# The last stage of a graph network: half of the second batch norm's scaling moved into TensorE's transposing matmuls, and half of the residual added by TensorE and kept in PSUM

## The chip, the cores and the metric

The kernel runs on one core of one Trainium2 chip. The metric is the device time of one execution in microseconds. Before the change it is 2655.15 us, the median of three runs (2654.74 to 2655.41). The profile is of one further execution, with a span of 2651.3 us; all points in time below count from the start of that span.

## The reference, cut to what matters

Sixteen batches of a 1024 x 256 array `x` pass through two layers. The first layer is attention over a graph with a layer norm at its end; its output is called x1 here, and the kernel keeps it in DRAM. The second layer, whose end is what is changed, is

```python
agg = einsum('nm,bmd->bnd', A_hat, x1)              # 1024 x 1024 adjacency
h   = relu(batchnorm(agg.reshape(-1, 256) @ W1.T + b1, g1, be1))   # 512 channels
out = h @ W2.T + b2                                 # 256 channels
out = batchnorm(out, g2, be2)                       # over all 16 * 1024 rows
y   = layernorm(x1 + out.reshape(16, 1024, 256))    # over the 256 channels of a row
```

The second batch norm needs its mean and variance over all rows of all batches, so nothing can be scaled before the last batch's `out` is there. After that every value of `out` is multiplied by a scale of its channel and gets a shift of its channel added, x1 is added, and each row is normalised over its 256 channels. Everything is in 32-bit floats.

## The kernel before, in words

The tail of the kernel has two stages. In both, the order of the instructions on TensorE (PE), ScalarE (ACT) and VectorE (DVE) is the order in which the program writes them (`manual_schedule`); GpSimd (POOL) and the DMA queue of SyncE (SP) are apart.

**Second linear layer (lines 1445 to 1468).** For each batch b and each half c of the 256 output channels, TensorE multiplies `w2T` with four chunks of h (`L1456`: two column halves for each of four chunks, eight matmul calls) into a PSUM tile `po2` with the channels on the partitions and the 1024 rows of the batch along the free dimension. VectorE moves it into SBUF as `o2T[b]` with the bias added (`L1460`) and takes the statistics with two bn_stats (`L1464`). After the last batch, `coefficients2(c)` aggregates the statistics (`L1227`, DVE) and works out the scale `sg2` and the shift `sh2` on GpSimd (`L587` to `L1231`), one column of each for each c. All of `o2T`, sixteen batches, stays in SBUF.

**Final stage (lines 1473 to 1542).** Per batch:

- `scale_shift` (`L1485`): ScalarE applies scale and shift in place, one 128 x 1024 activation for each of the two halves c.
- `residual2`: four pairs of 128-row blocks. For each pair TensorE transposes four 128 x 128 blocks into a PSUM bank (`L1497`), so that rows come onto the partitions and channels along the free dimension; VectorE adds x1 to it (`L1502`, 128 x 512, result in the tile `xf` in SBUF) and takes the statistics of both row blocks (`L1504`, 128 x 256 each). The four pairs go round four PSUM banks.
- ten small GpSimd instructions (`L1510` to `L1519`) turn these statistics into `rstd` and `nmr`, the scale and shift of each row.
- `finish`: ScalarE applies them in eight 128 x 256 activations (`L1526`), the result is stored by one 1 MB DMA (`L1530`), and the x1 of the batch seven later is loaded (`L1428`).

The written order is: `scale_shift(0)`, then for each b: `residual2(b)`, `scale_shift(b + 1)`, `finish(b - 1)`; and `finish(15)` at the end. So ScalarE prepares the next batch for TensorE and then finishes the batch before. x1 is loaded seven batches ahead.

Of the kernel before, what the change touches and what calls it, by code (L numbers as in the profile page):

```python
# [10 lines left out]
F32 = mybir.dt.float32  # L11
I32 = mybir.dt.int32
AF = mybir.ActivationFunctionType
ALU = mybir.AluOpType
AX = mybir.AxisListType
PSUM = bass.MemoryType.PSUM
DRAM = bass.MemoryType.DRAM

P = 128
HALF = 512  # L20
# [495 lines left out]
def fast_path(  # L516
# [19 lines left out]
    nc = tc.nc  # L536
    B, N, C = x.shape
    H = 4
    D = C // H
    NCH = N // P  # L540
    CC = C // P
    FH = W1.shape[0]
    HC = FH // P
    scale = float((1.0 + 1e-06) / (np.sqrt(D) + 1e-06))

    const = ctx.enter_context(tc.tile_pool(name="const", bufs=1))
# [4 lines left out]
    def open_psum():  # L551

        stack = ExitStack()
        for tag in "sto":
            psum[tag] = stack.enter_context(tc.tile_pool(name=f"ps_{tag}", bufs=2, space=PSUM))
        return stack
# [3 lines left out]
    def tile_s(name):  # L560
        return psum["s"].tile([P, N], F32, tag="s", name=name)

    def tile_t(name):
        return psum["t"].tile([P, HALF], F32, tag="t", name=name)

    def tile_o(name):
        return psum["o"].tile([P, HALF], F32, tag="o", name=name)
# [7 lines left out]
    ident = const.tile([P, P], F32, name="ident")  # L575
# [95 lines left out]
    H0, H1 = slice(0, HALF), slice(HALF, N)  # L671
# [3 lines left out]
    cols = {}  # L675
# [24 lines left out]
    with (  # L700
# [10 lines left out]
        st = {}  # L711
# [404 lines left out]
        with tc.manual_schedule(engines={mybir.EngineType.PE, mybir.EngineType.Activation, mybir.EngineType.DVE}):  # L1116
# [48 lines left out]
            for j in range(len(bursts)):  # L1165
                b, u = j // PERB, j % PERB
# [30 lines left out]
            j = len(bursts)  # L1197
# [14 lines left out]


    w1T, w2T = wl["w1T"], wl["w2T"]
    bn1_st = const.tile([P, HC, 2 * B, 6], F32, name="bn1_st")
    bn2_st = const.tile([P, CC, 2 * B, 6], F32, name="bn2_st")

    def batchnorm(stats, gamma, beta, k, name):

# [15 lines left out]
    with (  # L1235
# [9 lines left out]
        def bank(name):  # L1245
            return ps8.tile([P, HALF], F32, tag="bank", name=name)

        def temps(k):
            return lambda key, name: strt.tile([P, HALF], F32, tag=f"{key}{k}", name=f"{key}_{name}")


        wS = strt.tile([P, 4, C], F32, name="wS")
# [133 lines left out]
        def scale_shift1(h, k):  # L1386
            nc.scalar.activation(  # L1387
                h, h, AF.Relu, bias=sh1[:, k : k + 1], scale=sg1[:, k : k + 1]
            )
# [3 lines left out]
        for k in range(HC):  # L1393
            ps = [bank(f"ph_{k}_{half}") for half in range(2)]
            for c in range(CC):
                for half, hs in enumerate((H0, H1)):
                    nc.tensor.matmul(
                        ps[half], w1T[:, c, k * P : (k + 1) * P], t[:, c, hs],
                        start=(c == 0), stop=(c == CC - 1),
# [11 lines left out]
        nc.gpsimd.dma_start(h_d[B - 1], ht)  # L1411

    graph.close()
    ctx.enter_context(open_psum())

# [2 lines left out]
    with tc.tile_pool(name="o2p", bufs=1) as o2p:  # L1420
        o2T = [
            o2p.tile([P, CC, N], F32, tag=f"o2_{b}", name=f"o2_{b}") for b in range(B)
        ]
        xf = {}

        def load_x1(b, pool, tag):
            xf[b] = pool.tile([P, NCH, C], F32, tag=tag, name=f"xf_{b}")
            nc.sync.dma_start(xf[b], x1_d[b])  # L1428

        coefficients2, sg2, sh2 = batchnorm(bn2_st, cols["g2"], cols["be2"], CC, "bn2")  # L1430
        with (
            tc.tile_pool(name="hl", bufs=2) as hl,
            tc.manual_schedule(
                engines={mybir.EngineType.PE, mybir.EngineType.Activation, mybir.EngineType.DVE}
            ),
        ):
            hs_of = {0: h0}

            def load_h(b):
                ht = hl.tile([P, HC, N], F32, tag="hl", name=f"hl_{b}")  # L1440
                nc.sync.dma_start(ht, h_d[b])
                hs_of[b] = [ht[:, k, :] for k in range(HC)]

            load_h(1)
            for b in range(B):
                if b + 2 < B:
                    load_h(b + 2)
                if b + 1 < B:
                    for k in range(HC):
                        scale_shift1(hs_of[b + 1][k], k)  # L1450
                h = hs_of.pop(b)
                for c in range(CC):
                    ps = tile_s(f"po2_{b}_{c}")
                    for k in range(HC):
                        for hs in (H0, H1):
                            nc.tensor.matmul(  # L1456
                                ps[:, hs], w2T[:, k, c * P : (c + 1) * P], h[k][:, hs],
                                start=(k == 0), stop=(k == HC - 1),
                            )
                    nc.vector.tensor_scalar(  # L1460
                        o2T[b][:, c, :], ps, cols["b2"][:, c : c + 1], None, ALU.add
                    )
                    for half, hs in enumerate((H0, H1)):
                        nc.vector.bn_stats(bn2_st[:, c, 2 * b + half, :], o2T[b][:, c, hs])  # L1464
                    if b == B - 1:
                        coefficients2(c)
                if b >= B - 3:
                    load_x1(b - (B - 3), xp, "x")

        with (
            tc.tile_pool(name="fin2", bufs=4) as fin2,
            tc.manual_schedule(
                engines={mybir.EngineType.PE, mybir.EngineType.Activation, mybir.EngineType.DVE}
            ),
        ):
            for b in range(3, 7):
                load_x1(b, fin2, "xf")  # L1480

            def scale_shift(b):
                for c in range(CC):
                    o = o2T[b][:, c, :]
                    nc.scalar.activation(  # L1485
                        o, o, AF.Identity, bias=sh2[:, c : c + 1], scale=sg2[:, c : c + 1]
                    )

            def residual2(b):
                xt = xf[b]  # L1490
                st = small.tile([P, NCH, 6], F32, tag="ln_st", name=f"st_l1_{b}")
                for pair in range(NCH // 2):
                    pt = tile_t(f"pf_{b}_{pair}") if pair % 2 else tile_o(f"pf_{b}_{pair}")
                    for j in range(2):
                        n = 2 * pair + j
                        for c in range(CC):
                            nc.tensor.transpose(  # L1497
                                pt[:, j * C + c * P : j * C + (c + 1) * P],
                                o2T[b][:, c, n * P : (n + 1) * P], ident,
                            )  # L1500
                    xs = xt[:, 2 * pair : 2 * pair + 2, :].rearrange("p n c -> p (n c)")
                    nc.vector.tensor_add(xs, pt, xs)  # L1502
                    for n in (2 * pair, 2 * pair + 1):
                        nc.vector.bn_stats(st[:, n, :], xt[:, n, :])  # L1504

                me, qe, mo, qo = (st[:, :, k] for k in (1, 2, 4, 5))
                w = small.tile([P, 4, NCH], F32, tag="ln_w", name=f"w_l1_{b}")
                rstd, nmr, dif, var = (w[:, k, :] for k in range(4))
                pool = nc.gpsimd
                pool.tensor_tensor(nmr, me, mo, ALU.add)  # L1510
                pool.tensor_tensor(dif, me, mo, ALU.subtract)
                pool.tensor_tensor(var, qe, qo, ALU.add)
                pool.tensor_scalar(var, var, 1.0 / C, EPS, ALU.mult, ALU.add)
                pool.tensor_tensor(dif, dif, dif, ALU.mult)
                pool.tensor_scalar(dif, dif, 0.25, None, ALU.mult)
                pool.tensor_tensor(var, var, dif, ALU.add)
                pool.tensor_tensor(rstd, var, mhalf, ALU.pow)
                pool.tensor_tensor(nmr, nmr, rstd, ALU.mult)
                pool.tensor_scalar(nmr, nmr, -0.5, None, ALU.mult)  # L1519
                return rstd, nmr  # L1520

            def finish(b, rstd, nmr):
                xt = xf.pop(b)
                y = o2T[b].rearrange("p c n -> p (c n)").rearrange("p (n c) -> p n c", c=C)
                for n in range(NCH):
                    nc.scalar.activation(  # L1526
                        y[:, n, :], xt[:, n, :], AF.Identity,
                        bias=nmr[:, n : n + 1], scale=rstd[:, n : n + 1],
                    )
                nc.sync.dma_start(out[b].rearrange("(n p) c -> p n c", p=P), y)  # L1530
                if b + 7 < B:
                    load_x1(b + 7, *((fin2, "xf") if 3 <= b < 7 else (xp, "x")))

            scale_shift(0)
            coeffs = {}
            for b in range(B):
                coeffs[b] = residual2(b)
                if b + 1 < B:
                    scale_shift(b + 1)
                if b:  # L1540
                    finish(b - 1, *coeffs.pop(b - 1))
            finish(B - 1, *coeffs.pop(B - 1))


# [41 lines left out]
```

## Time and profile before

The final stage is the last 114 us of the span. A batch of it, as single rows and the timeline give it:

| engine | work of a batch | rows | time of a batch |
|---|---|---|---|
| ACT | 2 activations 128 x 1024, 8 of 128 x 256 | L1485 1226 ns, L1526 585 ns | 6.20 us from one batch to the next |
| DVE | 4 adds 128 x 512, 8 bn_stats 128 x 256 | L1502 677 ns, L1504 418 ns | 1.38 us for a pair, 5.5 us |
| PE | 16 transposes 128 x 128 | L1497 395 ns | 3 to 3.5 us in a row, then a wait |
| POOL | 10 small instructions | L1517 1667 ns, the others some 200 ns | 3.7 us |
| DMA | 1 MB in, 1 MB out | | 88% busy between 2555 and 2629 us |

The durations of single instructions overlap with the start of the next of the same engine, so the steps from start to start are shorter than these means: eight activations `L1526` take 4.03 us together, that is 0.49 us each.

For one logical fp32 matmul call the trace holds two records, each with a weight load of its own; for one `transpose` call it holds one. That is seen by counting. `L1456` is called 16 x 2 x 4 x 2 = 256 times and has 512 records; `L1497` is called 16 x 4 x 2 x 2 = 256 times and has 256 records.

### The profile page before, as it was taken

Reading aid. Unit: us, or ns where it says so; the run is one execution under the profiler, and the core shown is the slowest. Engines: PE = TensorE matmul, PEld = TensorE weight load, DVE = VectorE, ACT = ScalarE, POOL = GpSimd, SP = SyncE. Lnnn points to the kernel's source line nnn. Section 1 sums busy time; section 2 is a strip of 40 time slices with the busy share of each in tenths; the row PEclk is TensorE's granted clock in tenths of the full one; section 3 lists DMA queues with packets and bytes.
Section 4 is the critical chain, followed back from the end, with each engine's and each line's share of the span. In section 5 each row is a group of like instructions: output and inputs, shape, how many; then the busy total and the mean of one; then the engine's idle time right before and its main releaser. Section 6 shows DMA issues by size and latency. Waiting matters only on the chain. (4 is left out here: it accounts for less than half of the span.)

```text
span 2651.3 us, 31994 instructions
## 1 busy us (share of the span) xinstructions
PE 2553.7 (96%) x12966; PEld 1110.1 (42%) x12966; DVE 1600.2 (60%) x2160; ACT 1126.8 (43%) x1349; POOL 336.2 (13%) x407
## 2 busy tenths in 40 slices
PE   8999999999999999999999999999999999999964
PEld 4443444444434434444444343344444444444443
DVE  5465665756656657666566576765655655533376
ACT  5363563654645636545446354410101001233368
POOL 0001000100100011001000100321222211100044
PEclk9999999999999999999999999999999999999975
DMA  4001101001011011010110110112122122353367
GB/s 143 2 9 41 33 10 41 21 22 33 9 41 33 9 41 33 10 41 3 39 33 9 41 49 1 41 64 95 80 95 95 66 92 82 137 202 143 149 222 240
DMA packets 134557, 168.94 MB, mean 64 GB/s; under 512 B 86785, under 2 KB 120065, under 8 KB 124033
## 3 DMA queue, kind: packets, MB, share of 16 engines
q1 hardware_dynamic: 129568, 116.47, 14.2%
q0 software_dynamic: 4832, 50.34, 4.6%
q8 instruction: 103, 1.69, 0.3%
q14 instruction: 54, 0.43, 0.0%
HBM read 99.36 MB, written 67.44 MB: 63 GB/s over the span
## 5 line engine op out<-in xcount | busy, mean ns | idle before, releaser
L908 ACT ACTIVATE p<-ps 128x1024 f32<-128x1024 f32 x512 | 495.7, 1020 | 179.5 <-PE ps L903 142.9
L933 DVE TENSOR_TENSOR acc<-acc,p 128x1024 f32<-128x1024 f32 x384 | 483.2, 1258 | 61.0 <-ACT p L908 32.4
L903 PE MATMUL ps<-qT,kT 64*64 64x512 f32 x4096 | 490.6, 594 | 1.4 <-ACT p L908 1.4
L924 PE MATMUL po<-p,v 64*64 64x512 f32 x4096 | 485.3, 589 | 0.0
L805 PE MATMUL pg<-wg,x 128*128 128x512 f32 x960 | 425.2, 596 | 0.0
L979 POOL TENSOR_TENSOR x<-x,o 128x512 f32<-128x512 f32 x64 | 109.5, 1711 | 1434.8 <-DVE o L974 1434.8
L924 PEld LDWEIGHTS po<-p,v 64*64 64x64 f32 x4096 | 156.7, 133 | 282.8 <-issue 282.6
L805 PEld LDWEIGHTS pg<-wg,x 128*128 128x128 f32 x960 | 177.6, 190 | 226.9 <-issue 203.3
L903 PEld LDWEIGHTS ps<-qT,kT 64*64 64x64 f32 x4096 | 146.1, 132 | 280.2 <-issue 231.5
L817 ACT ACTIVATE qT<-qT 128x512 f32<-128x512 f32 x64 | 40.3, 631 | 482.0 <-DVE qT L814 481.9
L1456 PE MATMUL po<-hl,w12T 128*128 128x512 f32 x512 | 220.3, 592 | 3.1 <-ACT hl L1387 2.3
L814 DVE SCALAR_TENSOR_TENSOR qT<-pg,para_s 128x512 f32<-128x512 f32 x64 | 43.9, 689 | 271.1 <-PE pg L805 269.8
L793 DVE SCALAR_TENSOR_TENSOR wg<-wg,adj_s 128x1024 f32<-128x1024 f32 x128 | 153.1, 1217 | 15.5 <-ACT wg L789 15.5
L784 ACT ACTIVATE wg<-crow,ccol 128x1024 f32<-128x1024 f32 x128 | 146.6, 1146 | 11.8 <-DMA crow<-c 11.8
L1456 PEld LDWEIGHTS po<-hl,w12T 128*128 128x128 f32 x512 | 97.1, 190 | 126.3 <-issue 120.5
L789 ACT ACTIVATE wg<-wg 128x1024 f32<-128x1024 f32 x128 | 135.5, 1060 | 2.6
L1387 ACT ACTIVATE hl<-hl,bn_sh,bn_sg 128x1024 f32<-128x1024 f32 x64 | 74.3, 1229 | 135.0 <-DMA hl<-h 133.6
L855 PE MATMUL pv<-kvw_s,xT 128*128 128x256 f32 x512 | 124.0, 385 | 1.6 <-ACT kT L846 1.6
L1460 DVE TENSOR_SCALAR o<-po,col_b 128x1024 f32<-128x1024 f32 x32 | 41.1, 1284 | 139.1 <-PE po L1456 139.1
L842 PE MATMUL pk<-xT,kvw_s 128*128 128x512 f32 x256 | 120.3, 592 | 0.0
L855 PEld LDWEIGHTS pv<-kvw_s,xT 128*128 128x128 f32 x512 | 94.9, 190 | 51.9 <-issue 27.6
L1286 PE MATMUL a_agg<-ahT,x1l 128*128 128x512 f32 x240 | 108.1, 593 | 1.1 <-ACT agg L1104 1.1
(151 smaller groups left out, 2625.4 us busy)
## 6 DMA issues: line engine op xcount, KB each, us to landing
h<-hw POOLq DMA_DIRECT2D x16, 2048.0 KB, 6.6
hl<-h SPq DMA_DIRECT2D x15, 2048.0 KB
x<-x POOLq DMA_DIRECT2D x16, 1024.0 KB, 4.2
x1l<-x SPq DMA_DIRECT2D x16, 1024.0 KB
xf<-x SPq DMA_DIRECT2D x16, 1024.0 KB
out_dram<-o SPq DMA_DIRECT2D x16, 1024.0 KB
x<-in_x_dram SPq DMA_DIRECT2D x15, 1024.0 KB
crow<-c SPq DMA_DIRECT2D x15, 512.0 KB
```

The source lines that it names most:

```text
L784: nc.scalar.activation(w, s["crow"], AF.Abs, bias=s["ccol"][:, n : n + 1])
L789: nc.scalar.activation(w, w, AF.Tanh, scale=0.5)
L793: nc.vector.scalar_tensor_tensor(w, w, 1.0, adj_s[:, n, :], op0=ALU.subtract, op1=ALU.mult)
L805: nc.tensor.matmul(ps, xt[:, n, c * P : (c + 1) * P], s["wg", n][:, hs], start=(n == 0), stop=(n == NCH - 1),)
L842: nc.tensor.matmul(ps, kvw_s[:, c, kc * P : (kc + 1) * P], s["xT"][:, c, hs], start=(c == 0), stop=(c == CC - 1),)
L855: nc.tensor.matmul(pt[:, j * C : (j + 1) * C], s["xT"][:, c, n * P : (n + 1) * P], kvw_s[:, c, C : 2 * C], start=(c == 0), stop=(c == CC - 1),
L903: nc.tensor.matmul(ps[kh * D : (kh + 1) * D, hd * HALF : (hd + 1) * HALF], kT[r, pr, ks], qT[r, pr, qh * HALF : (qh + 1) * HALF], start=Tr ...
L908: nc.scalar.activation(p, ps, AF.Exp)
L924: nc.tensor.matmul(g["po"][kh][hd * D : (hd + 1) * D, :], s["v"][r, m, h * D : (h + 1) * D], p[r, hd * HALF : (hd + 1) * HALF], start=(m = ...
L933: nc.vector.tensor_add(g["acc"], g["acc"], p)
L979: nc.gpsimd.tensor_tensor(xs, xs, o.rearrange("p n h d -> p n (h d)"), ALU.add)
L1456: nc.tensor.matmul(ps[:, hs], w2T[:, k, c * P : (c + 1) * P], h[k][:, hs], start=(k == 0), stop=(k == HC - 1),)
```

## The change

It takes work off ScalarE and VectorE in the final stage and gives it to TensorE.

- **Scaling.** Only the channel half c = 0 is still scaled and shifted by ScalarE. For c = 1 the matmul that brings a block into row order has, in place of the identity, a diagonal matrix `dsg` of the scales. The shift of these channels comes from a matmul of a row of ones with the row of shifts (`one`, 1 x 128, and `row`, 1 x 256 for the two blocks of a pair), accumulated in the same PSUM bank. `dsg` and `row` are made once, in `shift_row`.
- **No more transpose calls.** Since the results accumulate, all sixteen block movements are now `nc.tensor.matmul` calls in place of `nc.tensor.transpose`, also those with the identity.
- **Residual.** For pairs 2 and 3 of each batch TensorE adds x1 by a matmul of the identity with x1 (`add_x1`, 512 columns), in the same bank. The sum stays in PSUM: bn_stats and the finishing activations of these four row blocks read it there. Pairs 0 and 1 are added by VectorE as before.
- **PSUM.** The pools of the stage before are closed; three tiles of two banks hold sums (`ps_held`), and pairs 0 and 1 go round two banks (`ps_sum`) where four pairs went round four.
- **The end of the linear layer.** The last tile of `out` (b = 15, c = 1) is moved by ScalarE in two halves in place of one VectorE instruction.

```diff
-                    nc.vector.tensor_scalar(
-                        o2T[b][:, c, :], ps, cols["b2"][:, c : c + 1], None, ALU.add
-                    )
+                    if b == B - 1 and c == CC - 1:
+                        for hs in (H0, H1):
+                            nc.scalar.activation(
+                                o2T[b][:, c, hs], ps[:, hs], AF.Identity,
+                                bias=cols["b2"][:, c : c + 1],
+                            )
+                    else:
+                        nc.vector.tensor_scalar(
+                            o2T[b][:, c, :], ps, cols["b2"][:, c : c + 1], None, ALU.add
+                        )
...
+        part_psum.close()
...
+            tc.tile_pool(name="ps_held", bufs=3, space=PSUM) as ps_held,
+            tc.tile_pool(name="ps_sum", bufs=2, space=PSUM) as ps_sum,
...
+            def shift_row():
+                nc.vector.tensor_scalar(dsg, ident, sg2[:, 1:2], None, ALU.mult)
+                pr = ps_sum.tile([P, HALF], F32, tag="sum", name="prow")
+                nc.tensor.matmul(pr[0:1, :P], sh2[:, 1:2], ident, start=True, stop=True)
+                for j in range(2):
+                    nc.vector.tensor_copy(row[:, j, :], pr[0:1, :P])
+
             def scale_shift(b):
-                for c in range(CC):
-                    o = o2T[b][:, c, :]
-                    nc.scalar.activation(
-                        o, o, AF.Identity, bias=sh2[:, c : c + 1], scale=sg2[:, c : c + 1]
-                    )
+                o = o2T[b][:, 0, :]
+                nc.scalar.activation(o, o, AF.Identity, bias=sh2[:, 0:1], scale=sg2[:, 0:1])
+
+            def add_x1(b, pair):
+                if b not in held:
+                    held[b] = ps_held.tile([P, N], F32, tag="held", name=f"held_{b}")
+                nc.tensor.matmul(
+                    held[b][:, (pair - 2) * HALF : (pair - 1) * HALF], ident,
+                    xf[b][:, 2 * pair : 2 * pair + 2, :].rearrange("p n c -> p (n c)"),
+                    start=True, stop=False, skip_group_check=True,
+                )
+
+            def transposed(b, pair, pt, start):
+                nc.tensor.matmul(
+                    pt.rearrange("p (n c) -> p n c", c=C)[:, :, P:], one, row,
+                    start=start, stop=False, skip_group_check=True,
+                )
+                for c in (1, 0):
+                    for j in range(2):
+                        n = 2 * pair + j
+                        nc.tensor.matmul(
+                            pt[:, j * C + c * P : j * C + (c + 1) * P],
+                            o2T[b][:, c, n * P : (n + 1) * P], dsg if c else ident,
+                            start=(start and c == 0), stop=True, skip_group_check=True,
+                        )
...
-                for pair in range(NCH // 2):
-                    pt = tile_t(f"pf_{b}_{pair}") if pair % 2 else tile_o(f"pf_{b}_{pair}")
-                    for j in range(2):
-                        n = 2 * pair + j
-                        for c in range(CC):
-                            nc.tensor.transpose(
-                                pt[:, j * C + c * P : j * C + (c + 1) * P],
-                                o2T[b][:, c, n * P : (n + 1) * P], ident,
-                            )
+                for pair in range(2):
+                    pt = ps_sum.tile([P, HALF], F32, tag="sum", name=f"pf_{b}_{pair}")
+                    transposed(b, pair, pt, True)
                     xs = xt[:, 2 * pair : 2 * pair + 2, :].rearrange("p n c -> p (n c)")
                     nc.vector.tensor_add(xs, pt, xs)
                     for n in (2 * pair, 2 * pair + 1):
                         nc.vector.bn_stats(st[:, n, :], xt[:, n, :])
+                for pair in range(2, 4):
+                    if b:
+                        add_x1(b, pair)
+                    pt = held[b][:, (pair - 2) * HALF : (pair - 1) * HALF]
+                    transposed(b, pair, pt, False)
+                    for j in range(2):
+                        nc.vector.bn_stats(st[:, 2 * pair + j, :], pt[:, j * C : (j + 1) * C])
...
+            add_x1(0, 2)
+            add_x1(0, 3)
             scale_shift(0)
+            shift_row()
```

`finish` takes the four blocks of pairs 2 and 3 first, from PSUM, then the other four from SBUF. Two tables of statistics, `bn1_st` and `bn2_st`, are moved to other SBUF pools.

## The prediction

> **What bounds the kernel now.** I first looked at the engines' busy time in stretches of the tail, because TensorE's 96% of the whole span says nothing of a stage in which it works otherwise. The columns are PE, weight loads, DVE, ACT, POOL, the granted TensorE clock, the DMA's share and its GB/s:
>
> ```profile
> 2531.70:2537.20 5.50, 0.21 (x1) 0.02 (x1) 3.58 (x4) 0.05 (x1) 1.36 (x5) 0.81 0.81 301
> 2537.20:2549.00 11.80, 7.64 (x43) 6.30 (x43) 9.38 (x21) 5.72 (x5) 3.44 (x10) 0.79 0.52 218
> ...
> 2555.00:2629.00 74.00, 44.60 (x192) 37.11 (x192) 65.65 (x145) 74.00 (x121) 41.26 (x120) 0.60 0.88 297
> 2629.00:2640.30 11.30, 2.65 (x16) 2.24 (x15) 6.50 (x15) 8.79 (x18) 6.87 (x20) 0.58 0.62 207
> 2640.30:2651.30 11.00, 0.00 (x0) 0.00 (x0) 0.00 (x0) 3.98 (x8) 0.00 (x0) 0.50 0.48 159
> ```
>
> From 2555 to 2629 us ScalarE is busy without a gap (74.00 of 74.00); TensorE is busy 60% of the time, and at a mean clock of 0.60. The chain of waits agrees: through this stretch it runs on ACT alone, and `L1526` starts at 2586.27 and again at 2592.47, so a batch costs **6.20 us**, which is eight `L1526` (0.49 each) and two `L1485` (1.13 each from start to start). Who waited for whom shows the other side:
>
> ```profile
> PE pf L1497 <- ACT o L1485: 40.4, 27, 6.5
> POOL w_l L1510 <- DVE st_l L1504: 40.2, 16, 8.0
> ```
>
> TensorE waits 40.4 us for the scaled tile. So taking one `L1485` of each batch away does shorten what paces the stage, as long as TensorE, which gets the work, stays under 6.20 us for a batch. Whether it does decides the case, so I price it from the timeline of TensorE (start, time to the last end, records):
>
> ```profile
> 1553.48 1.88 PE L842 MATMUL pk<-xT,kvw_s 128*128 128x512 f32 x4
> 1555.19 1.89 PE L855 MATMUL pv<-kvw_s,xT 128*128 128x256 f32 x8
> 1556.92 0.59 PE L842 MATMUL pk<-xT,kvw_s 128*128 128x512 f32 x1
> ...
> 1820.09 1.02 PE L1318 MATMUL c_h<-agg,wS 128*128 128x512 f32 x2
> 1821.05 0.19 PE L1343 MATMUL pgood<-top,ones 128*1 128x2 f32 x2
> 1821.16 2.41 PE L1286 MATMUL a_agg<-ahT,x1l 128*128 128x512 f32 x5
> ...
> 2544.26 0.66 PE L1497 MATMUL pf<-ident,o 128*128 128x128 f32 x4 [0.72 <-DVE xf L1502]
> 2555.42 3.46 PE L1497 MATMUL pf<-ident,o 128*128 128x128 f32 x15 [0.66 <-ACT o L1485]
> ```
>
> Four records of 512 columns step from 1553.48 to 1555.19: **0.429 us** a record. Eight of 256 columns step to 1556.92: **0.216 us**. The steps go with the columns, so 128 columns are 0.110; a single transpose record, also 128 columns, steps by 0.109 to 0.110 at full clock. At half clock (2555.42) it is (3.46 - 0.42) / 14 = 0.217. The middle three lines price a change of shape in the array: from the first `c_h` to `pgood` it is 0.96 us where two records would be 0.86, so some **0.093 us** are lost when a 128*1 weight follows a 128*128 one; on the way back 0.11 us pass from `pgood` to `a_agg`, of which the two little records use 0.03.
>
> **What the Trainium skill says.** "FP8 and Floating Point Precision", TensorE Precision Notes: true fp32 takes four passes through the array. The trace agrees: a matmul call is two records, each 512 columns in 0.429 us, which is 2.01 cycles a column at the page's 2.4 GHz; a transpose call is one. "Perfetto Trace Analysis", Optimizing Tensor Performance, Transposes: a logical transpose should be a transpose, not a standard matmul; the trace has both forms, at 1 and at 2 records a call. "TensorE: Matmul & The Clock Gate", step-by-step of a matmul: a weight load is pulled ahead of running matmuls unless row groups conflict; the 0.093 us at `pgood` fits a load that was not pulled ahead, though no 1-row weight occurs before. The same page, on the clock gate: the clock halves after an idle window of some 3.4 us and returns after a busy one; the 0.60 above is such a case.
>
> **The change part by part.** *ScalarE*: one `L1485` less a batch, 6.20 - 1.13 = 5.07 us. The activations reading PSUM I cost like those reading SBUF (copies from PSUM, `L937`, 586 ns for 512 columns; in SBUF, `L817`, 631 ns). *VectorE*: two pairs at 1.38 us as now, and four bn_stats from PSUM at 0.38 to 0.48 (the 0.418 of `L1504` and some for PSUM): 4.3 to 4.7 us in place of 5.5. *GpSimd* keeps its 3.7 us. *DMA* moves the same bytes.
>
> *TensorE*, a batch at full clock:
> - 16 block matmuls, each now two records: 32 x 0.110 = 3.52 us (before: 16 x 0.110 = 1.76).
> - 4 shift rows, 256 columns, two records: 8 x 0.216 = 1.73.
> - 2 `add_x1`, 512 columns, two records: 4 x 0.429 = 1.72.
> - 4 times into the 1-row weight of `one` and back: 8 x 0.093 = 0.74. This is the unknown: at best 0, since no 1-row weight is in the trace. I take the full value, because the three narrow kinds seen (128*1, 128*32, 64*64) all lose it beside 128*128.
>
> Sum **7.71 us** (6.97 without the last term). Weight loads: their records are 190 ns, longer than 110. I take them as hidden, because records of matmuls follow transposes after 0.109 us (`L765` to `L805`, 28 times) though their load is also recorded as 190. If they were not, 32 x 0.08 = 2.6 us would be added.
>
> So TensorE becomes the bound: 7.71 against ScalarE's 5.07 and the 6.20 that pace the stage now. Both waits that could stop it are covered: `scale_shift(b + 1)` waits on ACT behind `finish(b - 2)`, which waits for GpSimd some 5 us after TensorE has left batch b - 2, a batch and more before it is needed; and the third held tile is free long before. As it is busy without a break I take the full clock, but for one half-clock window at the start (1.7 us lost; 0 to 3.4).
>
> *The head.* The last matmul of `L1456` ends at about 2531.7. Before, `L1460` (1.29) and two `L1464` (1.30) follow; now the first ACT half can start on the first bank, and half a copy and two bn_stats lie in the chain: some 1.1 us less, so `sh2` comes at 2536.0 in place of 2537.1. Then, in place of a 1.25 us `L1485`, one small matmul, two copies of 1 x 128 and their waits: 0.8 to 1.5, I take 1.2. TensorE starts at 2537.2 (before 2538.45). `add_x1(0)` lies in the wait ahead of it; so does `dsg`.
>
> *The sum.* TensorE ends at 2537.2 + 16 x 7.71 - 1.72 + 1.7 = 2660.5. Two bn_stats and the end of the matmul follow (1.1): 2661.6. From the last bn_stats to the end it was 2635.8 to 2651.3 = 15.5 (GpSimd, eight activations, the last store) and stays so. The end is at 2677.1, against 2651.3: **+25.8 us, 2681.0 us**.
>
> **The rivals.**
> - *TensorE bound, the shift row costs nothing extra.* 16 x 0.74 = 11.8 less: 2669. For it: the load of a 1-row weight may go to a row group that is handled otherwise than a narrow column group.
> - *Weight loads exposed*, or the clock often at half. 16 x 2.6 = 41 more: 2722. Against: the 0.109 steps, and a clock of 1.0 wherever TensorE ran matmuls without a break.
> - *TensorE stays hidden, the kernel is faster.* If calls with a diagonal or identity cost one record like transposes, the batch would be some 4.3 us of TensorE and ScalarE would pace at 5.07. 13 of the saved `L1485` lie behind the first `finish`: 13 x 1.13 = 14.7, with 1.1 from the head, and some 2 given back at the end, where the last chain of TensorE, DVE and GpSimd (10.6 us from `scale_shift(15)` to `finish(15)`) doesn't shrink as much as ACT's work: 2641. For it: 40.4 us of waiting on TensorE. Against: every matmul call in the trace has two records.
>
> **How the numbers follow.** TensorE bound with the switches 0.56, without 0.22, loads exposed or a low clock 0.09, hidden 0.10, and 0.03 for a mixture that ends near no change. The prediction is the first, 2681. The range runs from the second less its cold start and a shorter head (2663) to the first with half a microsecond of waits in each batch and a little over (2697). Slower 0.87, same 0.03, faster 0.10.
>
> **What would show it.** In the changed profile TensorE should be busy near 100% from about 2537 to 2660 at clock 1.0; the block matmuls have 512 records, the rows 128, `add_x1` 64, and a batch 7.7 us from one to the next. ScalarE should fall to two thirds and wait for GpSimd, GpSimd for DVE, DVE for TensorE. A gap of 0.2 where `one` is loaded and no more than 0.110 between blocks confirm the terms. ScalarE still without gaps, or single records for the block matmuls, would prove me wrong.

## The result, and the profile after

The changed kernel takes 2718.64 us (median) against 2655.19 before: a ratio of 1.0238, 95% interval 1.0218 to 1.0258. It is **63.5 us slower**. One of the four timed runs, 2778.02 us at a lower mean clock (0.968 against 0.992 and 0.993), was in a slower state and is left out of the ratio. The direction was forecast and so was the engine that becomes the bound; the size was not: 25.8 us were predicted, and the range ended at 2697.

The stretches of the tail, read as before (PE, weight loads, DVE, ACT, POOL, granted clock, DMA share, GB/s), with who waited for whom after them (in total, times, longest):

```profile
2540.00:2560.00 20.00, 19.15 (x66) 13.11 (x65) 7.30 (x16) 4.05 (x9) 3.47 (x10) 0.57 0.17 72
2560.00:2580.00 20.00, 18.29 (x96) 11.74 (x94) 8.82 (x20) 6.91 (x13) 6.86 (x20) 1.00 0.61 201
...
2680.00:2700.00 20.00, 18.29 (x96) 11.74 (x94) 8.82 (x20) 8.82 (x17) 6.86 (x20) 1.00 0.32 107
```

```profile
ACT o L1575 <- POOL w_l L1568: 97.2, 16, 21.0
DVE st_l L1553 <- PE held L1531: 66.3, 32, 3.3
...
PE held L1517 <- DVE st_l L1553: 12.8, 15, 0.9
```

ScalarE, which had no gap before, now idles 97.2 us in the stage; VectorE waits 66.3 us for TensorE; the DMA share falls from 88% to between 61% and 65% from 2560 to 2640 us. So TensorE is the bound. But it isn't busy without a break: 18.29 of 20 us, and in the first stretch its clock is 0.57. The third wait says who stops it, 15 times (in batch 0, whose `add_x1` ran ahead, the shift matmul of pair 3 waits instead). One batch of the timeline, from the first shift matmul of pair 0 to that of the next batch, shows all of it (TensorE's lines, and VectorE's one that matters):

```profile
2603.23 0.69 PE L1524 MATMUL pf<-row,one 1*128 1x256 f32 x2
...
2603.86 0.71 PE L1531 MATMUL pf<-dsg,o 128*128 128x128 f32 x4
...
2604.40 0.61 PE L1531 MATMUL pf<-ident,o 128*128 128x128 f32 x4
...
2604.94 0.69 PE L1524 MATMUL pf<-row,one 1*128 1x256 f32 x2
...
2608.69 0.61 PE L1531 MATMUL held<-ident,o 128*128 128x128 f32 x4
2609.34 0.76 DVE L1553 BATCH_NORM_STATS2 st_l<-held 128x6 f32<-128x256 f32 x2 [1.10 <-PE held L1531]
...
2610.15 1.12 PE L1517 MATMUL held<-xf,ident 128*128 128x512 f32 x2 [0.85 <-DVE st_l L1553]
...
2611.21 0.69 PE L1524 MATMUL held<-row,one 1*128 1x256 f32 x2
...
2612.92 0.69 PE L1524 MATMUL pf<-row,one 1*128 1x256 f32 x2
```

From 2603.23 to 2612.92 a batch takes **9.69 us**, not 7.71. The records are the forecast ones: two for each matmul call, four in the `dsg` group and four in the `ident` group of a pair. Two things are larger. A shift matmul starts at 2603.23 and the block after it at 2603.86, 0.63 us for two records whose columns take 0.43. And `add_x1` of pair 3 starts at 2610.15, just after VectorE has finished the statistics of pair 2 (2609.34 + 0.76), though it writes another bank. The starts of single records give the terms of the batch:

| term | predicted us | measured us | how measured |
|---|---|---|---|
| 32 block records | 3.52 | 3.58 | 0.112 from one to the next |
| 8 shift records, columns | 1.73 | 1.73 | 0.216 where nothing else delays them (second experiment) |
| 4 add_x1 records | 1.72 | 1.72 | 0.431 and 0.429 |
| change of the weight's shape | 0.74 | 1.56 | at each shift matmul four steps too long: 0.205 for 0.110 into it, 0.320 for 0.216 between its records, 0.304 for 0.216 behind it, 0.213 for 0.112 between the first two block records |
| wait for VectorE | 0 | 1.12 | 1.129 in place of 0.111 into the second add_x1, 0.533 in place of 0.431 within it |
| sum | 7.71 | 9.71 | 9.69 from batch to batch |

The head did not go as forecast either:

```profile
2528.54 3.17 PE L1457 MATMUL po<-hl,w12T 128*128 128x512 f32 x7
...
2530.34 3.50 ACT L1510 ACTIVATE o<-o,bn_sh,bn_sg 128x1024 f32<-128x1024 f32 x3 [13.14 <-POOL bn_sh L1229]
...
2533.75 1.24 ACT L1463 ACTIVATE o<-po,col_b 128x512 f32<-128x512 f32 x2
2534.44 1.29 DVE L1472 BATCH_NORM_STATS2 bn_st<-o 128x6 f32<-128x512 f32 x2 [5.91 <-ACT o L1463]
...
2538.36 0.19 POOL L1229 TENSOR_TENSOR bn_sh<-col_be,bn_sh 128x1 f32<-128x1 f32 x1
...
2539.56 0.69 PE L1524 MATMUL pf<-row,one 1*128 1x256 f32 x2 [0.57 <-DVE row L1506]
```

TensorE's last linear matmul ends at 2531.7, but the two ACT halves (`L1463`) start at 2533.75. On ACT they stand behind three `scale_shift` activations, of batches 0, 1 and 2: across the two stages the order of the built program is not that of the text. The shift is there at 2538.55, not at 2536.0, and TensorE starts at 2539.56, not at 2537.2. From 2542.1 to 2559.1 it then runs at half clock, 17.1 us, where one window of 3.4 was forecast. It is busy for 95% of that time:

```profile
2542.06:2559.13 17.07, 16.22 (x51) 11.15 (x51) 6.62 (x16) 3.18 (x7) 3.47 (x10) 0.50 0.08 32
```

### The profile page after: what moved, and what is told of

It reads as the page before. It is cut to its first block, busy times and chain, and to the rows that moved or that the text cites. A ratio compares the mean times of both kernels' runs of the same rounds, so it can differ in the third digit from the quotient of the medians.

```text
span 2716.0 us, 32806 instructions
## 1 busy us (share of the span) xinstructions
PE 2648.1 (97%) x13416; PEld 1158.0 (43%) x13416; DVE 1583.0 (58%) x2130; ACT 1108.2 (41%) x1335; POOL 336.1 (12%) x408
## 5 line engine op out<-in xcount | busy, mean ns | idle before, releaser
L924 PE MATMUL po<-p,v 64*64 64x512 f32 x4096 | 485.3, 589 | 0.0
L805 PE MATMUL pg<-wg,x 128*128 128x512 f32 x960 | 425.2, 596 | 0.0
L924 PEld LDWEIGHTS po<-p,v 64*64 64x64 f32 x4096 | 156.7, 133 | 282.8 <-issue 282.6
L805 PEld LDWEIGHTS pg<-wg,x 128*128 128x128 f32 x960 | 177.6, 190 | 226.9 <-issue 203.3
L1286 PE MATMUL b_agg<-aT,x1S 128*128 128x512 f32 x240 | 109.2, 598 | 0.0
```

Of the source, the lines that this page charges most:

```text
L805: nc.tensor.matmul(ps, xt[:, n, c * P : (c + 1) * P], s["wg", n][:, hs], start=(n == 0), stop=(n == NCH - 1),)
L924: nc.tensor.matmul(g["po"][kh][hd * D : (hd + 1) * D, :], s["v"][r, m, h * D : (h + 1) * D], p[r, hd * HALF : (hd + 1) * HALF], start=(m = ...
L1286: nc.tensor.matmul(ps, left, right, start=(start and i == 0), stop=(i == NCH // 2 - 1), skip_group_check=True,)
```

## The experiments

The question was where 38 us beyond the forecast come from. My theory: the wait on the shared two-bank tile, the change of shape, and the clock. The main rival: the weight loads of all short records are exposed. It had given 2722 before the run, nearly what was measured, so the total alone speaks for it; only the 0.112 between block records speaks against.

**One-bank tiles for the held sums.**

```diff
-            tc.tile_pool(name="ps_held", bufs=3, space=PSUM) as ps_held,
+            tc.tile_pool(name="ps_held", bufs=6, space=PSUM) as ps_held,
...
-                    held[b] = ps_held.tile([P, N], F32, tag="held", name=f"held_{b}")
+                held[b, pair] = ps_held.tile([P, HALF], F32, tag="held", name=f"held_{b}_{pair}")
```

> The held sums lie in six tiles of one bank in place of three tiles of two banks; nothing else changes. Theory W (of the 9.69 us that a batch takes in the changed kernel, 1.12 are add_x1 of pair 3 waiting for the two bn_stats of pair 2, and the wait hangs on the shared two-bank tile): the wait is gone, a batch takes 8.57 us, 16 x 1.12 = 18 us less, about 2701. Rival L (weight loads of the 128-column records are exposed, as the rival of the prediction that gives 2722): no change, 2719. Rival V (TensorE waits for VectorE because VectorE is late, whatever the tile): the wait moves to the next matmul and the time stays within 4 us of 2719.

Measured: 2702.87 us, ratio to before 1.0183 (1.0166 to 1.0200), 15.8 us less than the changed kernel. The timeline of TensorE around pair 3:

```profile
2604.90 0.61 PE L1530 MATMUL held<-ident,o 128*128 128x128 f32 x4
2605.35 1.02 PE L1516 MATMUL held<-xf,ident 128*128 128x512 f32 x2
```

`add_x1` (now `L1516`) follows the last block of pair 2 after 0.45 us, the four block records, and no wait is left. A batch takes 8.57 us (the finishing activations of neighbouring batches start at 2613.01 and 2621.58), as the theory has it. The half clock at the start lasted 20.5 us here, 3.4 more, which takes back some 2 of the 16 x 1.12 = 17.9 us: the first two batches take 24.9 us in both kernels. So the wait was on the tile, not on VectorE's pace.

**Ones of 128 rows for the shift.**

```diff
-            row = o2p.tile([1, 2, P], F32, name="row")
-            one = o2p.tile([1, P], F32, name="one")
+            row = o2p.tile([P, 2, P], F32, name="row")
+            one = o2p.tile([P, P], F32, name="one")
...
-                pr = ps_sum.tile([P, HALF], F32, tag="sum", name="prow")
-                nc.tensor.matmul(pr[0:1, :P], sh2[:, 1:2], ident, start=True, stop=True)
                 for j in range(2):
-                    nc.vector.tensor_copy(row[:, j, :], pr[0:1, :P])
+                    nc.vector.tensor_scalar(row[:, j, :], ident, sh2[:, 1:2], None, ALU.mult)
```

> The shift comes from a 128 x 128 matrix of ones times a diagonal of the shifts, twice side by side, in place of a 1 x 128 row of ones times a 1 x 256 row: the same 256 columns and the same number of matmuls, but no weight of one row. Theory S (a change of the weight's shape exposes four weight loads of 0.1 us at each of the 4 shift matmuls of a batch, 1.56 us in all): the four steps fall to 0.216 and 0.112, a batch takes 8.13 us, about 25 us less, 2694; if the 1-row matmuls are also what keeps the clock at half from 2542 to 2559 us, up to 8 us less again, 2686. Rival L (weight loads exposed everywhere): 2719, since the number of loads is the same.

Measured: 2685.60 us, ratio 1.0121 (1.0104 to 1.0138), 33.0 us less. The steps are 0.112 into a shift matmul, 0.218 between its records, 0.216 behind it: the four lost tenths are gone, with the same number of records and of loads. That refutes the exposed loads and confirms that the matmuls with one row cost this time. The losses come in pairs, at the record after each change of shape and at the one behind it; that a weight load is exposed there was not seen by itself. A batch takes 8.14 us. And the clock:

```profile
2540.00:2560.00 20.00, 17.38 (x108) 14.50 (x108) 12.18 (x28) 6.50 (x13) 6.93 (x20) 0.98 0.31 101
```

It is 0.98 in the stretch where the changed kernel has 0.57. The one half-clock period now lies at 2533.8 to 2540.6, where TensorE mostly waits for the coefficients. But not all of the 33 us belongs to the stage. The linear layer ends at 2529.5 here:

```profile
2528.51 1.02 PE L1457 MATMUL po<-hl,w12T 128*128 128x512 f32 x2
```

In the profile of the changed kernel it ends at 2531.7; that profile has one more half-clock window, at 1760 us, worth some 1.7 us by its length of 3.4, in a part of the program that the edit doesn't touch. Whether each timed run differs so is not shown. Of the 32.6 us between the two profiled spans, 24.8 are the shape (16 x 1.55 from batch to batch), 2.2 lie ahead of the stage, and some 5.6 are left for the clock and the shorter start of the stage.

**Both.**

> Both changes together: one-bank held tiles, and 128-row ones for the shift. Theory (TensorE's matmul columns alone remain, 6.97 to 7.05 us a batch): 16 x 2.68 = 43 us less than 2718.6, about 2676, and 2668 if the clock also comes back early; still slower than before (2655), because 7.0 is above the 6.2 us of a batch there. Rival L: 2719 or little less. Rival A (with these gone ScalarE or the chain to GpSimd paces at 6 us or less): about 2655 or faster.

Measured: 2668.00 us, ratio 1.0054 (1.0037 to 1.0071). TensorE's timeline of a batch, from pair 0 to pair 0 of the next (7.02 us from `finish` to `finish`):

```profile
2607.06 0.60 PE L1521 MATMUL pf<-row,one 128*128 128x256 f32 x2
2607.50 0.61 PE L1528 MATMUL pf<-dsg,o 128*128 128x128 f32 x4
2607.94 0.61 PE L1528 MATMUL pf<-ident,o 128*128 128x128 f32 x4
2608.39 0.60 PE L1521 MATMUL pf<-row,one 128*128 128x256 f32 x2
...
2611.89 1.02 PE L1514 MATMUL held<-xf,ident 128*128 128x512 f32 x2
```

A shift matmul and its eight blocks take 2608.39 - 2607.06 = 1.33 us, which is 2 x 0.216 + 8 x 0.112. Nothing but columns is left, TensorE is busy 20.00 of 20 us, and the kernel is still slower than before: seven microseconds of matmul columns are more than the 6.20 that ScalarE had needed. This is the core of the forecast by itself, without the wait and the change of shape. (In this profile too the linear layer ends early, at 2529.4 against 2531.7 before, so the stage itself lost more than the total says.)

**No shift.** The held tiles have one bank, and the shift of c = 1 is left out altogether.

> One-bank held tiles, and the shift of the channel half c = 1 is left out (no shift matmul; the scale of these channels stays). Theory: the shift matmuls cost 1.73 (columns) + 1.56 (change of shape) = 3.29 us of a batch, so a batch takes 8.57 - 3.29 = 5.28 us on TensorE, just above ScalarE's 5.07: 2701 - 53 = 2648 or a little less with an earlier full clock. Rival L: 8 of 44 weight loads fewer, 2719 less some 15. If the time is well above 2655 something other than TensorE paces the stage.

Measured: 2641.24 us, ratio 0.9951 (0.9934 to 0.9968). A batch takes 5.29 us as forecast; with one short half-clock window in place of 20.5 us the stage is 8 us ahead of my estimate. So without the shift matmuls, and with one-bank tiles, the change would pay. The run also shows that the DMA would not have been the limit: it moves 400 to 403 GB/s here while TensorE is busy 20.00 of 20 us.

**Transposes where nothing is added** (on top of both changes): the c = 0 blocks of pairs 0 and 1.

```diff
+                        if start and c == 0:
+                            nc.tensor.transpose(
+                                pt[:, j * C : j * C + P], o2T[b][:, 0, n * P : (n + 1) * P], ident
+                            )
+                            continue
```

> As the kernel with one-bank held tiles and 128-row ones (2668.0), but the blocks of c = 0 in pairs 0 and 1, to which nothing is added on TensorE, are moved by transpose again. Theory P (a matmul call is two records of 0.110 us, a transpose call one): four calls of a batch lose 0.110 us each, 7.0 - 0.44 = 6.57 us a batch, 16 x 0.44 = 7 us less, 2661. Rival (a switch between transpose and matmul costs as much as it saves, two switches a pair at 0.1): 2668.

Measured: 2661.48 us, ratio 1.0028 (1.0016 to 1.0040), 6.5 us less than with both changes. The two transposes of a pair are two records where the matmuls were four, at 0.109 each, and the switch between the forms costs nothing (0.109 to 0.112 either way).

**The last tile by VectorE again** (the changed kernel otherwise).

> The changed kernel with the last tile of the linear layer moved by VectorE in one instruction, as before the change. Theory H (in the changed kernel the two ACT halves stand behind three scale_shift activations on ACT and start 2.1 us after TensorE's last matmul, so the last shift is there at 2538.55 us in place of 2537.13): undoing it brings the shift back to about 2537.1, 1.4 us less, and add_x1(0) starts some 2 us earlier: 2717 against 2718.6. Rival (the move to ACT helps, as the prediction had it): 1.1 us more, 2719.7.

Measured: 2718.70 us, ratio 1.0242 (1.0229 to 1.0256): no difference, where 2717 was expected. The earlier start was there:

```profile
2531.64 1.28 DVE L1468 TENSOR_SCALAR o<-po,col_b 128x1024 f32<-128x1024 f32 x1 [3.21 <-PE po L1457]
...
2536.88 0.19 POOL L1229 TENSOR_TENSOR bn_sh<-col_be,bn_sh 128x1 f32<-128x1 f32 x1
...
2538.07 0.85 PE L1524 MATMUL pf<-row,one 1*128 1x256 f32 x2 [0.57 <-DVE row L1506]
```

The shift is there at 2537.07 and TensorE starts 1.5 us earlier. But the clock is halved from 2538.5 and comes back at 2559.0, the same moment as in the changed kernel; TensorE works through more of that stretch, at half speed, and the gain of the head is gone by its end. That reading fits the two traces; it was not tried apart.

**Only the scaling** on TensorE: diagonal for c = 1, 128-row ones, transposes for c = 0, VectorE adds all pairs and moves the last tile.

> Only the scaling goes to TensorE: c = 1 by the diagonal, the shift by 128-row ones, c = 0 by transposes; all four pairs are added by VectorE from four one-bank tiles, no add_x1, and the last tile of the linear layer goes by VectorE. Theory: TensorE 8 x 0.110 + 16 x 0.112 + 8 x 0.216 = 4.4 us, ScalarE 5.07, VectorE 5.5 of a batch, so VectorE paces at 5.5 against 6.20 before: 14 x 0.7 = 10 us faster than before, 2645. Rival D (the DMA, 88% busy at 6.2 us a batch, holds the pace): 2650 to 2655. Rival T (TensorE at half clock for much of the stage because it is busy only 80%, 8.8 us there): 2665 or more.

Measured: 2648.60 us, ratio 0.9979 (0.9970 to 0.9987), **6.1 us faster than before** (2654.68 in the same rounds), where 10 were expected. VectorE paces as forecast, at 5.58 us a batch (19.3 of 20 us busy). TensorE, busy for 16 to 17 of 20 us, keeps a clock of 1.00 from 2560 to 2620, so the rival of the half clock is out for most of the stage; and the next kernel, at 4.98 us a batch, shows that the DMA does not hold this pace. In the profiled run TensorE is at half clock for 6.8 us from 2538.4, and for 3.4 us at 2326.7, so that the linear layer ends 1.8 us later; whether each timed run has that is not shown.

**One pair added by TensorE, the shift in bf16.**

```diff
+            rows = [o2p.tile([P, 2, P], BF16, name=f"row{i}") for i in range(2)]
+            one = o2p.tile([P, P], BF16, name="one")
...
+                for i, row in enumerate(rows):
+                    nc.tensor.matmul(
+                        pt.rearrange("p (n c) -> p n c", c=C)[:, :, P:], one, row,
+                        start=(start and i == 0), stop=False, skip_group_check=True,
+                    )
...
-                for pair in range(2, 4):
+                for pair in range(3, 4):
```

> As the one before, but x1 of pair 3 alone is added by TensorE and kept in PSUM, and the shift is made by two bf16 matmuls (the shift split in a bf16 part and a bf16 rest, with 128-row bf16 ones) in place of one fp32 matmul of two records. Theory: a bf16 matmul of 256 columns is one record of half the steps, 0.107 us, so TensorE has 6 x 0.11 + 2 x 0.22 + 16 x 0.112 + 8 x 0.107 + 0.86 = 4.6 us, VectorE 3 x 1.38 + 0.77 = 4.9, ScalarE 5.0: ScalarE and the DMA pace at 5.1: 14 x 1.1 = 15 us faster than before, 2640. Rival: change of the data type exposes weight loads, 8 x 0.1 more, 5.4 on TensorE, 2645.

Measured: 2637.50 us, ratio 0.9935 (0.9922 to 0.9947): **17.2 us faster than before** (2654.68). It beats both kernels. The two edits, the pair and the bf16 shift, were not run apart. A batch takes 4.98 us. One pair of it on TensorE:

```profile
2586.30 0.38 PE L1528 MATMUL pf<-row,one 128*128 128x256 bf16 x2
2586.52 0.61 PE L1540 MATMUL pf<-dsg,o 128*128 128x128 f32 x4
2586.97 0.38 PE L1536 MATMUL pf<-ident,o 128*128 128x128 f32 x2
2587.19 1.02 PE L1520 MATMUL held<-xf,ident 128*128 128x512 f32 x2
```

Two bf16 records of 256 columns take 2586.52 - 2586.30 = 0.22 us. So a bf16 call costs 0.11 us where an fp32 call of as many columns cost 0.43; the whole pair takes 0.89 us where the changed kernel needed 1.71. ScalarE is back at 20.00 of 20 us:

```profile
2580.00:2600.00 20.00, 19.39 (x145) 16.01 (x144) 19.23 (x46) 20.00 (x38) 13.72 (x40) 1.00 1.05 402
```

## Why the prediction was wrong

**Right, and why.** ScalarE paced the stage before, and one `L1485` less of a batch was a true gain: the last experiment collects it. TensorE became the bound because a matmul call is two records where a transpose is one, and because shift and residual add columns of their own: the record counts and the steps 0.112, 0.216 and 0.431 came as priced from the rows of before, and with wait and shape change taken out the kernel stands at 2668.0, against the 2669 of the rival without shape changes. That it comes so close is partly luck, since in that profile the linear layer ended 2.3 us earlier than before. That weight loads are hidden beside 128 columns held too: 0.112 us from record to record, with loads recorded as 190 ns and more. The two pages of the Trainium skill on the passes ("FP8 and Floating Point Precision", TensorE Precision Notes, and "Perfetto Trace Analysis", Transposes) fit: an fp32 call of 256 columns took 0.43 us and a bf16 one 0.11, and four calls of a batch turned back into transposes gave 6.5 us. (The 2.4 GHz that the prediction gives beside the first of them stand in "TensorE: Matmul & The Clock Gate".)

**Wrong**, in the order of size, for the profiled runs (16 batches):

1. *"Both waits that could stop it are covered."* There was a third: `add_x1` of pair 3 writes the tile whose other bank VectorE reads for the statistics of pair 2. 16 x 1.12 = 17.9 us (in batch 0, at half clock, the wait is 0.92). I had looked for waits between batches, and not at a tile with two users within one. One-bank tiles took it away.
2. *"4 times into the 1-row weight of `one` and back: 8 x 0.093"*: the mechanism was right, the term mis-sized. A shift matmul loses four steps, not two, because its second record and the second block record behind it start late too: 1.56 in place of 0.74, 16 x 0.82 = 13.1 us. I had read one step at each change around `pgood`. Half of what was missing stood in the line behind it: five `a_agg` records take 2.41 us, of which 0.59 are the last one's own, so the four steps are 1.82 and not 4 x 0.429 = 1.72. It is the second record that comes late (0.533 in place of 0.429), and so it does in all 32 returns from 64*64 to 128*128 weights in the profile of before (`L924` to `L805`).
3. *"But for one half-clock window at the start (1.7 us lost)"*: 17.1 us at half clock. The first two batches took 11.45 and 13.46 us; at full clock they would have taken 7.97 (9.69 less the 1.72 of `add_x1`, which ran ahead) and 9.69. So 7.2 us were lost, 5.5 more than counted. The Trainium skill, "TensorE: Matmul & The Clock Gate", on the clock gate, says that a busy window of some 3.4 us brings the full clock, and I relied on it; here five windows with TensorE busy 95% of the time did not, so the measurement decides. With 128-row ones 6.8 us were the most.
4. *"Some 1.1 us less"* in the head: the ACT halves came late, TensorE started at 2539.56 in place of 2537.2, 2.4 us. I had taken ACT's order from the text across a border between two stages. The profile of before showed that an `L1485` can run ahead of the linear layer's end (batch 0, at 2530.29), but no work of that layer stood behind it on ACT. This term is not independent of the third: with an earlier start the half clock took the gain back (sixth experiment).
5. Block records of 0.112 in place of 0.110: 1 us.

Together 39.9 us; with the 25.8 predicted 65.7, against the 64.7 by which the profiled spans differ. Of the 1.0 too much, 0.6 is the stretch from TensorE's last record to the end, which took 16.0 us in place of 16.6; the rest is not assigned.

On the third step, the low clock before the change was not the case of idle windows that the prediction took it for. The clock stood at half for 27.3 us on end, and between 2555 and 2629 us no wait of TensorE was longer than 2.4 us:

```profile
2593.18:2620.49 27.31, 17.77 (x76) 14.99 (x74) 23.87 (x52) 27.31 (x46) 15.87 (x48) 0.50 0.85 286
...
PE pf L1497 <- ACT o L1485: 29.6, 24, 2.4
```

The range failed for the same reasons: it took the shape term from 0 to 0.74 us, half a microsecond of waits in a batch where 1.12 came, and a cold start of one window at most.

## What to carry to other kernels

Before work is moved to a second engine, count its records and columns in the same trace and set the sum against the pace of the stage, not against the idle time of the engine: here 40 us of idle TensorE had room for the scaling, not for scaling, shift and residual in fp32. Moving the part that fits, as transposes where nothing accumulates and with weights of full height, turned a loss of 63 us into a gain of 17. And look for two users of one tile inside an iteration: two banks in one tile can be one wait, two tiles are none.

## What the hardware showed that was not expected

- A matmul with a 1-row weight, 128 columns wide, between 128-row ones delays four records by about 0.09 to 0.10 us each (0.205, 0.320, 0.304, 0.213 where 0.112, 0.218, 0.216, 0.112 stand with 128 rows): at each change of shape the first record and the one behind it.
- The three kernels of the changed form with 1-row weights kept half the clock for 17.1 to 20.5 us of nearly unbroken matmuls in their profiles; with 128-row ones it was 3.4 to 6.8 us (6.8 in the kernel with both changes, 20.5 in the one that differs from it by the 1-row weights alone). Why is open.
- Reading PSUM cost these engines little: bn_stats 423 ns from PSUM, 418 from SBUF; finishing activations 563 from PSUM, 600 from SBUF.
- A change from fp32 to bf16 weights of the same shape cost nothing: 0.109 us on either side.
